# Edge counting moved between expert outputs and attention weights, expert rows added without order, x read back in chunks

## The chip, the cores and the metric

The kernel runs on one core of one Trainium2 chip. The metric is the device time of one execution in microseconds. Before the change the median of three executions is 2445.32 us (2440.54 to 2446.48).

## The reference

The model is four layers on a graph of N = 2708 nodes with D = 256 features and a dense 0/1 adjacency matrix. Each layer adds a graph part and then a feed-forward part to x, each on a layer norm of x:

```python
x = x + _L0_gnn_ref(ln(x), adj, ...)   # cosine attention over neighbours
x = x + _L0_ffn_ref(ln(x), ...)        # slice tokens and a small state-space scan
x = x + _L1_gnn_ref(ln(x), adj, ...)   # mean of neighbours, one linear map
x = x + _L1_ffn_ref(ln(x), ...)        # 8 experts, top 2, 256 -> 1024 -> 256
x = x + _L2_gnn_ref(ln(x), adj, W, a)  # graph attention, one head, elu
x = x + _L2_ffn_ref(ln(x), ...)        # 4 experts, scores from attention over an edge list
x = x + _L3_gnn_ref(ln(x), adj, W, a)  # graph attention, four heads
x = x + _L3_ffn_ref(ln(x), ...)        # 8 experts, top 1, with a capacity
```

The parts that matter here are the feed-forward of layer 1, the graph attention of layer 2, and one input of layer 2's feed-forward:

```python
# layer 1 feed-forward: a token's output is the weighted sum of its two experts
top_w, top_i = top_k(xf @ Wg + bg, 2); top_w = softmax(top_w)
out += w_dense[:, e:e+1] * (gelu(xf @ W1[e] + b1[e]) @ W2[e] + b2[e])

# layer 2 graph attention
wh = h @ W
e = leaky_relu(wh @ a1 + (wh @ a2).T, 0.2), masked by adj
h_prime = elu(softmax(e) @ wh)

# layer 2 feed-forward, scores: a segment softmax over 1,048,576 edges
src, dst = edge_index        # numbers below 65536, of which N are nodes here
```

Edge numbers are drawn below 65536, so only few edges have a destination among the 2708 nodes. The kernel has to find these edges in the list before layer 2's feed-forward.

## The kernel before

All of x stays in SBUF as 22 tiles of 128 rows (the last has 20). TensorE (PE) does the matrix products; VectorE (DVE) the layer-norm statistics, attention weights and copies; ScalarE (ACT) Gelu, exponentials and copies; GpSimd (POOL) starts the indirect DMAs; SyncE (SP) starts the plain loads. A scheduler fixes the order of instructions on each engine when the kernel is built: each engine then goes through its list in order, and an instruction that waits holds up what stands behind it. The order comes from the position in the program, which acts as a priority, and from the scheduler's own estimate of when operands are ready.

*Start.* The first four tiles of x are loaded singly, two by SP and two by ACT, then the rest in pieces of four or five tiles. `CHUNKS` are six pieces of 512 columns (the last of 148).

*Layer 1's feed-forward* (`fast_l1_ffn`). `Route` picks two experts for each token and writes, for every expert, a list of at most 768 rows (six tiles). An indirect DMA gathers an expert's rows (xe, L2954). Each expert is done in two halves of three tiles. A half is turned (xT: PE transposes, and copies from PSUM by `k.copy`, which alternates DVE, L76, and ACT, L78), goes up (h_ps, L3242, Gelu by ACT, L3249) and down (y_ps, L3259). DVE adds the bias and multiplies by the gate (ys, L3267 and L3268), and POOL adds the tile into rows of `acc` in DRAM by an indirect DMA (L3271). The adds write the same tensor, so each waits until the one before has landed. Rows of the lists that hold no token go to 128 spare rows behind the N + 1 rows of `acc`. PSUM has three banks for h_ps and two for y_ps. When all is added, x is read back from `acc` by SP.

*The edge search* (`Edges.search`, L2566 to L2590). The edge list is cut into eight pieces of 128x1024. For each piece DVE makes keys, then takes the eight largest of each row nine times (MAX8, L2585; the replacement, L2586), and reduces what is left (L2589). One piece is offered after each expert; the scheduler spreads the instructions between the outputs of experts, from 835 to 1065 us.

*The edge count* (`Edges.count`). A first part splits the found keys into node and row numbers, ranks the edges that are left over (rank_oh, L2686, rank_ov on POOL, L2701, 32 matmuls, L2708), and prepares `hib` and `lob`. Then 18 steps compare these with an iota: `oh` (128x4096, L2749), `ol` (128x704) and 32 small matmuls (L2756) that sum counts into cnt_ps. These steps are in the attention of layer 2, four after each chunk of columns; the scheduler moved the first part and two of the 18 steps up into the features before it.

*Layer 2's attention* (`fast_gat`, H = 1). First layer norm (L1617 to L1631), transposes (ft_ps, L1587), the features V and the two attention values of each node (v_ps, L3389; fs, L3399), an extreme of them (gx), and a spread of R over partitions (Rr). Then for each chunk of 512 target columns and each of 21 row tiles j: DVE makes PT (L3459), and PE does four matmuls (L3528) into four accumulators. PT has ten buffers, the adjacency tiles eight.

Of the kernel before, what the change touches and what calls it, by code (L numbers as in the profile page):

```python
# [1 line left out]

# [5 lines left out]
F32 = mybir.dt.float32  # L8
# [4 lines left out]
ALU = mybir.AluOpType  # L13
AX = mybir.AxisListType
PSUM = bass.MemoryType.PSUM
DRAM = bass.MemoryType.DRAM

N = 2708
# [25 lines left out]
class K:  # L44
# [3 lines left out]
    def __init__(self, ctx, tc, x_in):  # L48
        self.tc = tc
        self.nc = nc = tc.nc  # L50
        self.flip = 0
        pool = ctx.enter_context(tc.tile_pool(name="shared", bufs=1))
        self.x = pool.tile([128, NT, D], F32, name="x")
        nc.vector.memset(self.x[:, NT - 1, :], 0.0)
        for t in range(4):
            (nc.scalar if t % 2 else nc.sync).dma_start(
                self.x[:, t, :], x_in[t * 128 : (t + 1) * 128]
            )
        for t0, n in ((4, 4), (8, 4), (12, 4), (16, 5)):
            nc.sync.dma_start(  # L60
                self.x[:, t0 : t0 + n, :],
                x_in[t0 * 128 : (t0 + n) * 128].rearrange("(t p) d -> p t d", p=128),
            )
        nc.sync.dma_start(self.x[:TAIL, NT - 1, :], x_in[(NT - 1) * 128 : N])
# [5 lines left out]
        nc.vector.memset(self.eps, 1e-5)  # L70

    def copy(self, out, in_):
# [2463 lines left out]
class Edges:  # L2536
# [55 lines left out]
    def count(self):  # L2592
        nc, tc = self.k.nc, self.k.tc
        with tc.tile_pool(name="ep", bufs=1) as pp, tc.tile_pool(
            name="eh", bufs=2
        ) as hot, tc.tile_pool(name="ps_eh", bufs=1, space=PSUM) as ps:
            ioi = pp.tile([128, 128], I16, name="ioi")
# [51 lines left out]
            nc.vector.tensor_scalar(before, ioi, pc, None, ALU.is_gt)  # L2649
            rp = ps.tile([128, 5 * OW], F32, name="rank_ps")  # L2650
            bp = rp[:, 4 * OW : 4 * OW + 1]
# [91 lines left out]
            yield  # L2743
            cp = ps.tile([128, NT], F32, name="cnt_ps")
            for s0 in range(0, LW, HB):
# [89 lines left out]
class Route:  # L2835
# [14 lines left out]
    def __init__(self, k, ctx, w, most):  # L2850
# [9 lines left out]
        self.fd = dram.tile([N + 1, self.W], F32, name="fd")  # L2860
        self.acc = dram.tile([N + 1 + 128, D], F32, name="acc")
        self.idg = keep.tile([128, S], I32, name="idg")
# [66 lines left out]
        nc.vector.tensor_scalar(self.p1, self.own[:, 0:1], 1.0, None, ALU.add)  # L2929
        self.p1n = pool.tile([128, 1], F32, name="p1n")  # L2930
        nc.vector.tensor_scalar(self.p1n, self.p1, float(N), None, ALU.add)
        self.slot_f = pool.tile([128, 3, S], F32, name="slot_f")
# [31 lines left out]
    def early(self):  # L2964

        v = self.k.nc.vector
        bad = self.k.bad[:, 6:7]
        v.tensor_scalar(bad, self.sofar[:, 0:1], -1.0, float(HT * 128), ALU.mult, ALU.add)
        f = self.one.tile([128, 2, HT], F32, name="early_f")
        idf, idp = f[:, 0, :], f[:, 1, :]  # L2970
        v.scalar_tensor_tensor(
            idf, self.slot_f[:, 1, :HT], 128.0, self.slot_f[:, 2, :HT], ALU.mult, ALU.add
        )
        self.number(idf, idp, self.idg0, self.ids0)
        self.xe0 = self.gather(self.idg0, self.most * 128 + 1)
        yield

    def number(self, idf, idp, idg, ids):

        v = self.k.nc.vector  # L2980
# [217 lines left out]
def fast_l1_ffn(k, side, route, rest):  # L3198
# [8 lines left out]
    with ExitStack() as ctx:  # L3207
        dp = ctx.enter_context(tc.tile_pool(name="f1a", bufs=4))
        op = ctx.enter_context(tc.tile_pool(name="f1o", bufs=6))
        pst = ctx.enter_context(tc.tile_pool(name="ps_f1t", bufs=2, space=PSUM))  # L3210
        ps1 = ctx.enter_context(tc.tile_pool(name="ps_f11", bufs=3, space=PSUM))
        ps2 = ctx.enter_context(tc.tile_pool(name="ps_f12", bufs=2, space=PSUM))

        def psum():
            return pst.tile([128, 512], F32, name="xt_ps")

        class Half:
# [36 lines left out]
            def down(self):  # L3254
                _, _, w2t, b2t = route.weights[self.e]
                for i in range(HT):
                    y = ps2.tile([128, D], F32, name="y_ps")
                    for m in range(M):
                        nc.tensor.matmul(  # L3259
                            y,  # L3260
                            lhsT=self.hT[:, m, i * 128 : (i + 1) * 128],
                            rhs=w2t[:, m, :],
                            start=(m == 0),
                            stop=(m == M - 1),
                        )
                    ys = op.tile([128, D], F32, name="ys")
                    nc.vector.tensor_tensor(ys, y, b2t, ALU.add)  # L3267
                    nc.vector.tensor_scalar(  # L3268
                        ys, ys, self.xe[:, i, D + self.e : D + self.e + 1], None, ALU.mult
                    )  # L3270
                    nc.gpsimd.indirect_dma_start(  # L3271
                        out=acc,
                        out_offset=bass.IndirectOffsetOnAxis(
                            ap=self.ids[:, i : i + 1], axis=0
                        ),
                        in_=ys,
                        in_offset=None,
                        compute_op=ALU.add,
                    )
                    yield  # L3280

# [23 lines left out]
        route.slots()  # L3305
        side = side(route.start)
        nxt = [one, half(0, 1)]
        run(first)
        for e in range(E):
# [16 lines left out]
        for t0 in range(0, NT - 1, 3):  # L3326
            nc.sync.dma_start(
                k.x[:, t0 : t0 + 3, :],
                acc[1 + t0 * 128 : 1 + (t0 + 3) * 128].rearrange(
                    "(t p) d -> p t d", p=128  # L3330
                ),
            )
        nc.sync.dma_start(k.x[:TAIL, NT - 1, :], acc[1 + (NT - 1) * 128 : 1 + N])


def fast_gat(k, adjT, W, a, H, elu, col, side, parts=CHUNKS, after=None):
# [10 lines left out]
    with ExitStack() as ctx:  # L3347
# [109 lines left out]
        def product(PT, R, Q, aj):  # L3457

            nc.vector.scalar_tensor_tensor(PT, R, Q, aj, ALU.max, ALU.mult)  # L3459

        def weights(c0, cs, j, h, aj):

            PT = ptp.tile([128, 512], F32, name="PT")
            product(PT[:, :cs], Rr[:, h, c0 : c0 + cs], Q[:, h, j : j + 1], aj[:, :cs])
            return PT
# [51 lines left out]
        for i, (c0, cs) in enumerate(parts):  # L3517
            if H == 1:
# [24 lines left out]
                for (t, o, n), ac in zip(bl, acc):  # L3543
# [876 lines left out]
def part(I, prefix):  # L4420
    return {n[len(prefix) :]: ap for n, ap in I.items() if n.startswith(prefix)}


def model(tc, I, out):
# [4 lines left out]
    with tc.tile_pool(name="flags", bufs=1) as fp:  # L4429
# [4 lines left out]
        with ExitStack() as ctx:  # L4434
            k = Fast(ctx, tc, I["x"], bad, adjT)
            with ExitStack() as c0:
                pooling = Pooling(k, part(I, "L0_ffn_"), c0)
                fast_l0_gnn(k, adjT, I["L0_gnn_WqkT"], pooling)
                fast_l0_ffn(k, part(I, "L0_ffn_"), pooling)
            with tc.tile_pool(name="lists", bufs=1) as lp:  # L4440
                edges = Edges(k, part(I, "L2_ffn_"), lp)
                order = (0, 1, 5, 2, 3, 4)
                with ExitStack() as c1:
# [17 lines left out]
                    )  # L4461
                    fast_l1_ffn(k, edges.search, route, rest)
                fast_gat(
                    k, adjT, I["L2_gnn_W"], I["L2_gnn_a"], 1, True, 2, edges.count()
                )
# [75 lines left out]
```

## Time and profile before

The profiled execution took 2441.02 us; its span is 2439.3 us. Stages of the span, from the windows of the trace:

| stage | us | PE busy | DVE busy | TensorE clock |
|---|---|---|---|---|
| layer 0, graph part | 0 to 370 | 352.0 | 174.1 | 1.00 |
| layer 0, feed-forward | 370 to 600 | 206.7 | 147.9 | 0.90 |
| layer 1, graph part | 600 to 790 | 182.5 | 93.0 | 0.98 |
| layer 1, experts | 790 to 1165 | 355.1 | 269.7 | 0.98 |
| read-back and features of layer 2 | 1165 to 1233 | 36.7 | 51.8 | 0.76 |
| layer 2, attention | 1233 to 1456 | 220.5 | 207.6 | 0.99 |
| layer 2, feed-forward | 1456 to 1740 | 271.7 | 95.3 | 0.93 |
| layer 3, attention | 1740 to 2165 | 407.6 | 373.2 | 0.98 |
| layer 3, feed-forward | 2165 to 2439 | 227.8 | 124.7 | 0.90 |

A stage in which PE's busy time is near its length is bound by PE. A stage in which it isn't has waits, and the list of waits says for what. The clock is the share of full speed that TensorE was granted in the stage. In the profile's lines, `PE ft_ps L1587 <- DVE fa L1631: 19.1, 1, 19.1` means that PE, at the instruction that writes ft_ps on line 1587, waited for DVE's fa of line 1631: 19.1 us in total, once, 19.1 at the longest. A line of the timeline gives the start, the duration, the engine, the line, the operation, output and input, their shapes, how many instructions are merged, and in brackets the idle time before with what ended it.

### The profile page before, as it was taken

What the parts mean: (1) busy time and instruction counts of PE and PEld (TensorE: products, weight loads), DVE (VectorE), ACT (ScalarE), POOL (GpSimd) and SP (SyncE); (2) the same over time, 40 slices, a digit from 0 to 9 for tenths busy, and PEclk for the clock granted to TensorE, in tenths of its full rate; (3) what the DMA queues carried; (4) which work ended last, traced back from release to release, by engine and by line L of the source; (5) the groups of instructions that cost most, each with busy time, mean ns of one, the idle gap of its engine ahead of it and who ended that gap; (6) DMA issues with size and microseconds to landing.
All of it is one profiled execution on the core that took longest, in us unless ns stands there. A gap on an engine that the chain in (4) does not pass through costs nothing. (4 is left out here: it accounts for less than half of the span.)

```text
span 2439.3 us, 31809 instructions
## 1 busy us (share of the span) xinstructions
PE 2260.7 (93%) x11620; PEld 1509.5 (62%) x11620; DVE 1537.2 (63%) x3419; ACT 658.6 (27%) x1329; POOL 418.5 (17%) x490
## 2 busy tenths in 40 slices
PE   7999999988999899999599999999889999968997
PEld 4677775677877667767478867666653333325664
DVE  6444338655355699951698993252579999853544
ACT  5433333214663222121310013232321111111121
POOL 2000003005000333432150002520030000002221
PEclk9999999889999899999889996999899999978998
DMA  4233322200673444341254423000024443314340
GB/s 129 65 99 96 100 61 77 74 1 15 217 236 108 140 119 124 84 89 18 63 167 138 135 54 58 21 1 1 10 71 116 115 115 111 92 50 164 117 133 14
DMA packets 158380, 219.34 MB, mean 90 GB/s; under 512 B 30879, under 2 KB 94083, under 8 KB 158212
## 3 DMA queue, kind: packets, MB, share of 16 engines
q1 hardware_dynamic: 125856, 179.58, 25.7%
q0 software_dynamic: 15248, 23.39, 4.8%
q10 hardware_dynamic: 17108, 14.22, 1.8%
q8 instruction: 96, 1.57, 0.3%
q14 instruction: 72, 0.59, 0.1%
HBM read 193.49 MB, written 24.17 MB: 89 GB/s over the span
## 5 line engine op out<-in xcount | busy, mean ns | idle before, releaser
L3459 DVE SCALAR_TENSOR_TENSOR PT<-Rr,Q,aj 128x512 f32<-128x512 f32 (+3 forms) x630 | 406.1, 709 | 25.8 <-PE acc_ps L3528 13.9
L3605 PE MATMUL acc_ps<-PT,V 128*64 128x512 f32 (+4 forms) x2016 | 328.5, 549 | 0.4 <-ACT Rr L78 0.4
L3605 PEld LDWEIGHTS acc_ps<-PT,V 128*64 128x64 f32 (+1 forms) x2016 | 95.2, 122 | 210.2 <-issue 154.6
L1819 PE MATMUL acc_ps<-fa,PT 128*128 128x257 f32 x882 | 214.0, 382 | 0.5 <-DVE PT L1793 0.5
L1819 PEld LDWEIGHTS acc_ps<-fa,PT 128*128 128x128 f32 x882 | 164.6, 190 | 63.8 <-issue 41.0
L3528 PE MATMUL acc_ps<-V,PT 128*128 128x257 f32 x882 | 199.0, 385 | 1.5 <-POOL V L3416 0.9
L3528 PEld LDWEIGHTS acc_ps<-V,PT 128*128 128x128 f32 x882 | 167.6, 192 | 28.7 <-DVE PT L3459 2.4
L3242 PE MATMUL h_ps<-xT,w1t 128*128 128x384 f32 x512 | 173.4, 497 | 6.1 <-DVE xT L76 5.6
L1793 DVE SCALAR_TENSOR_TENSOR PT<-aj,PT 128x512 f32<-128x512 int32 (+1 forms) x126 | 80.2, 644 | 147.7 <-ACT PT L1792 147.6
L3259 PE MATMUL y_ps<-w2t,hT 128*128 128x256 f32 x768 | 168.6, 379 | 0.0
L2478 PE MATMUL acc_ps<-V,at 128*128 128x257 bf16 x1323 | 156.6, 277 | 3.7 <-DVE at L2472 3.7
L3259 PEld LDWEIGHTS y_ps<-w2t,hT 128*128 128x128 f32 x768 | 145.4, 190 | 21.4
L2478 PEld LDWEIGHTS <-at 128*128 128x128 bf16 x1323 | 129.4, 99 | 26.0 <-issue 5.0
L3242 PEld LDWEIGHTS h_ps<-xT,w1t 128*128 128x128 f32 x512 | 97.5, 194 | 73.9 <-DVE xT L76 7.3
L1792 ACT ACTIVATE PT<-s_ps,rq 128x512 f32<-128x512 f32 (+1 forms) x126 | 79.3, 636 | 168.1 <-PE s_ps L1768 167.0
L3271 POOL DMA_INDIRECT acc<-ys,ids x48 | 78.8, 1641 | 239.7 <-DVE ys L3268 114.1
L1768 PE MATMUL s_ps<-KT,QT 128*128 128x512 f32 (+1 forms) x252 | 116.4, 546 | 0.9 <-POOL KT L1747 0.6
L3951 PE MATMUL y_ps<-w2t,hT 128*128 128x256 f32 (+1 forms) x528 | 117.2, 379 | 0.0
L3938 PE MATMUL h_ps<-fT,w1t 128*128 128x512 f32 (+1 forms) x288 | 116.3, 554 | 0.1
L4374 PE MATMUL y_ps<-w2t,hT 128*128 128x256 f32 (+1 forms) x512 | 112.8, 379 | 0.0
L3951 PEld LDWEIGHTS y_ps<-w2t,hT 128*128 128x128 f32 (+1 forms) x528 | 97.7, 186 | 22.3 <-issue 8.2
L3249 ACT ACTIVATE hT<-h_ps,b1t 128x384 f32<-128x384 f32 x128 | 74.3, 580 | 110.3 <-PE h_ps L3242 107.8
(743 smaller groups left out, 3353.3 us busy)
## 6 DMA issues: line engine op xcount, KB each, us to landing
aj<-in_adjT SPq DMA_DIRECT2D x399, 256.0 KB
w1t<-in_L_ffn_W SPq DMA_DIRECT2D x8, 1024.0 KB
w2t<-in_L_ffn_W SPq DMA_DIRECT2D x8, 1024.0 KB
w1t<-in_L_ffn_w SPq DMA_DIRECT2D x8, 1024.0 KB
w2t<-in_L_ffn_w SPq DMA_DIRECT2D x8, 1024.0 KB
aj<-in_adjT SPq DMA_DIRECT2D x63, 74.0 KB
fd<-fa ACTq DMA_DIRECT2D x9, 512.0 KB
aj<-in_adjT SPq DMA_DIRECT2D x21, 202.0 KB
```

The lines of the kernel that those rows point to most:

```text
L1768: nc.tensor.matmul(s[:, :cs], lhsT=QT[:, j * 128 : j * 128 + 128], rhs=KT[:, c0 : c0 + cs], start=True, stop=True,)
L1793: nc.vector.scalar_tensor_tensor(PT[p, :n], aj[p, :n], 0.0, PT[p, :n], ALU.is_gt, ALU.mult)
L1819: nc.tensor.matmul(ac, lhsT=PT[:, o : o + n], rhs=fa[:, j, :], start=j == 0, stop=False)
L2478: nc.tensor.matmul(ac[:, c:], lhsT=at[:, o : o + n], rhs=V[:, j, r], start=j == 0 and q == 0, stop=False, skip_group_check=True,)
L3242: nc.tensor.matmul(hp, lhsT=w1t[:, kk, m * 128 : (m + 1) * 128], rhs=self.xT[:, kk, :], start=(kk == 0), stop=(kk == 1),)
L3259: nc.tensor.matmul(y, lhsT=self.hT[:, m, i * 128 : (i + 1) * 128], rhs=w2t[:, m, :], start=(m == 0), stop=(m == M - 1),)
L3459: nc.vector.scalar_tensor_tensor(PT, R, Q, aj, ALU.max, ALU.mult)
L3528: nc.tensor.matmul(ac[:n], lhsT=PT[:, o : o + n], rhs=V[:, j, 0, :], start=(j == 0), stop=False,)
L3605: nc.tensor.matmul(w.pop("out"), **w)
L3938: nc.tensor.matmul(o[:, :cs], lhsT=w1t[:, kk, m * 128 : (m + 1) * 128], rhs=fT[:, kk, c0 : c0 + cs], start=(kk == 0), stop=(kk == 1),)
L3951: nc.tensor.matmul(y[:n], lhsT=hT[:, m, o : o + n], rhs=w2t[:, m, :], start=(m == 0), stop=(m == M - 1),)
L4374: nc.tensor.matmul(y[:n], lhsT=hT[:, m, o : o + n], rhs=w2t[:, m, :], start=(m == 0), stop=(m == M - 1),)
```

## The change

1. `load_x` loads x at the start and reads it back after layer 1, in six pieces as `CHUNKS` has them (the last with a load of its own for the 20 rows). From the third on, each waits for the landing of the one two before it. All are on SP.
2. The adds of one expert are declared independent of each other; the first of an expert waits for all of the expert before; the read-back waits for the adds of the last expert. The spare rows of `acc` become 768, one for each row of a list, and are zeroed by six DMAs.
3. In layer 1's experts, h_ps has two PSUM banks and y_ps three. The copies of xT are all on ACT.
4. Search and count are one chain of steps. After experts 0 to 7 come 1, 1, 2, 1, 2, 1, 3 and 2 steps, each placed, by `tc.issue_after`, behind the last ys of that expert: eight of the search, the count's first part and four of the 18. The other 14 are in the attention, each behind the PT of every fifth row tile. The tiles of the count lie on the other side of the memories, and ranks and counts share one PSUM bank.

```diff
@@ Kernel
+        self.load_x(lambda r: x_in[r])
...
+    def load_x(self, src, also=None):
+        ld = []
+        for c0, cs in CHUNKS:
+            t0, n = c0 // 128, cs // 128
+            ld.append(
+                self.nc.sync.dma_start(
+                    self.x[:, t0 : t0 + n, :],
+                    src(slice(c0, c0 + n * 128)).rearrange("(t p) d -> p t d", p=128),
+                )
+            )
...
+        for i, inst in enumerate(ld):
+            if also:
+                also(inst)
+            if i > 1:
+                self.tc.add_manual_dep(
+                    inst.ins,
+                    ld[i - 2].ins.name,
...
@@ Route
-        nc.gpsimd.dma_start(self.acc[N + 1 :, :], zero[:, :D])
+        for i in range(TPE):
+            nc.gpsimd.dma_start(self.acc[N + 1 + i * 128 : N + 129 + i * 128, :], zero[:, :D])
...
-        v.tensor_scalar(idp, idf, 0.0, self.p1n, ALU.is_equal, ALU.mult)
+        spare = self.spare.rearrange("p e t -> p (e t)")[:, : idf.shape[1]]
+        v.scalar_tensor_tensor(idp, idf, 0.0, spare, ALU.is_equal, ALU.mult)
@@ fast_l1_ffn
-        ps1 = ctx.enter_context(tc.tile_pool(name="ps_f11", bufs=3, space=PSUM))
-        ps2 = ctx.enter_context(tc.tile_pool(name="ps_f12", bufs=2, space=PSUM))
+        ps1 = ctx.enter_context(tc.tile_pool(name="ps_f11", bufs=2, space=PSUM))
+        ps2 = ctx.enter_context(tc.tile_pool(name="ps_f12", bufs=3, space=PSUM))
...
-                    k.copy(self.xT[:, kk, :], tp[:, :HC])
+                    nc.scalar.copy(self.xT[:, kk, :], tp[:, :HC])
...
+                    mine = adds.setdefault(self.e, [])
+                    for o in mine:
+                        tc.declare_no_dep(add.ins, o.ins, reason="rows of other tokens")
+                    if not mine:
+                        wait_for(add, adds.get(self.e - 1, []))
+                    mine.append(add)
...
-            next(side)
-        for _ in side:
-            pass
...
+            with tc.issue_after(now[-1].last.ins):
+                for _ in range((1, 1, 2, 1, 2, 1, 3, 2)[e]):
+                    next(side)
+        k.load_x(lambda r: acc[1 + r.start : 1 + r.stop], lambda ld: wait_for(ld, adds[E - 1]))
@@ fast_gat
+                    if j % 5 == 4:
+                        with tc.issue_after(made[0].ins):
+                            next(side, None)
...
-                for _ in range(4):
-                    next(side, None)
```

More of the change, by code (lines that the diff above doesn't have):

```diff
@@ L1 @@
 from contextlib import ExitStack
+from itertools import chain
 import concourse.bass as bass
@@ L54, in __init__ @@
         nc.vector.memset(self.x[:, NT - 1, :], 0.0)
[L55 to L64, printed above, removed]
+        self.load_x(lambda r: x_in[r])
         self.ident = pool.tile([128, 128], F32, name="ident")
@@ L70, in __init__ @@
         nc.vector.memset(self.eps, 1e-5)
+    def load_x(self, src, also=None):
[8 more added lines that the diff above has]
+            )
+            if cs % 128:
+                ld.append(
+                    self.nc.sync.dma_start(
+                        self.x[:TAIL, NT - 1, :], src(slice((NT - 1) * 128, N))
+                    )
+                )
+        for i, inst in enumerate(ld):
[5 more added lines that the diff above has]
+                    ld[i - 2].ins.name,
+                    mybir.DependencyInfo(
+                        mybir.DependencyClass.Sync, mybir.DependencyReason.DATA
+                    ),
+                    reason="the first are to land first",
+                )
     def copy(self, out, in_):
@@ L2593, in count @@
         nc, tc = self.k.nc, self.k.tc
-        with tc.tile_pool(name="ep", bufs=1) as pp, tc.tile_pool(
-            name="eh", bufs=2
-        ) as hot, tc.tile_pool(name="ps_eh", bufs=1, space=PSUM) as ps:
+        with tc.tile_pool(name="ep", bufs=1, side="right") as pp, tc.tile_pool(
+            name="eh", bufs=2, side="right"
+        ) as hot, tc.tile_pool(name="ps_eh", bufs=1, space=PSUM, side="right") as ps:
+            bank = ps.tile([128, 512], F32, name="edge_ps")
             ioi = pp.tile([128, 128], I16, name="ioi")
@@ L2649, in count @@
             nc.vector.tensor_scalar(before, ioi, pc, None, ALU.is_gt)
-            rp = ps.tile([128, 5 * OW], F32, name="rank_ps")
+            rp = bank[:, : 5 * OW]
             bp = rp[:, 4 * OW : 4 * OW + 1]
@@ L2743, in count @@
             yield
-            cp = ps.tile([128, NT], F32, name="cnt_ps")
+            cp = bank[:, 5 * OW : 5 * OW + NT]
             for s0 in range(0, LW, HB):
@@ L2860, in __init__ @@
         self.fd = dram.tile([N + 1, self.W], F32, name="fd")
-        self.acc = dram.tile([N + 1 + 128, D], F32, name="acc")
+        self.acc = dram.tile([N + 1 + TPE * 128, D], F32, name="acc")
         self.idg = keep.tile([128, S], I32, name="idg")
@@ L2929, in __init__ @@
         nc.vector.tensor_scalar(self.p1, self.own[:, 0:1], 1.0, None, ALU.add)
-        self.p1n = pool.tile([128, 1], F32, name="p1n")
-        nc.vector.tensor_scalar(self.p1n, self.p1, float(N), None, ALU.add)
+        self.spare = count("spare", [E, TPE], [[0, E], [128, TPE]], base=N + 1, mult=1)
         self.slot_f = pool.tile([128, 3, S], F32, name="slot_f")
@@ L2966, in early @@
         v = self.k.nc.vector
-        bad = self.k.bad[:, 6:7]
-        v.tensor_scalar(bad, self.sofar[:, 0:1], -1.0, float(HT * 128), ALU.mult, ALU.add)
+        first = self.sofar[:, 0:1]
+        v.tensor_scalar(first, first, float(HT * 128), None, ALU.max)
         f = self.one.tile([128, 2, HT], F32, name="early_f")
@@ L3210, in fast_l1_ffn, with wait_for @@
         pst = ctx.enter_context(tc.tile_pool(name="ps_f1t", bufs=2, space=PSUM))
-        ps1 = ctx.enter_context(tc.tile_pool(name="ps_f11", bufs=3, space=PSUM))
-        ps2 = ctx.enter_context(tc.tile_pool(name="ps_f12", bufs=2, space=PSUM))
+        ps1 = ctx.enter_context(tc.tile_pool(name="ps_f11", bufs=2, space=PSUM))
+        ps2 = ctx.enter_context(tc.tile_pool(name="ps_f12", bufs=3, space=PSUM))
         def psum():
             return pst.tile([128, 512], F32, name="xt_ps")
+        adds = {}
+        def wait_for(inst, others):
+            for o in others:
+                tc.add_manual_dep(
+                    inst.ins,
+                    o.ins.name,
+                    mybir.DependencyInfo(
+                        mybir.DependencyClass.Sync, mybir.DependencyReason.DATA
+                    ),
+                    reason="all of an expert's rows",
+                )
         class Half:
@@ L3267, in down @@
                     nc.vector.tensor_tensor(ys, y, b2t, ALU.add)
-                    nc.vector.tensor_scalar(
+                    self.last = nc.vector.tensor_scalar(
                         ys, ys, self.xe[:, i, D + self.e : D + self.e + 1], None, ALU.mult
                     )
-                    nc.gpsimd.indirect_dma_start(
+                    add = nc.gpsimd.indirect_dma_start(
                         out=acc,
@@ L3305, in fast_l1_ffn @@
         route.slots()
-        side = side(route.start)
+        side = iter(side(route.start))
         nxt = [one, half(0, 1)]
@@ L3322, in fast_l1_ffn @@
                 k.checked()
-            next(side)
-        for _ in side:
-            pass
[L3326 to L3333, printed above, removed]
+            with tc.issue_after(now[-1].last.ins):
+                for _ in range((1, 1, 2, 1, 2, 1, 3, 2)[e]):
+                    next(side)
+        k.load_x(lambda r: acc[1 + r.start : 1 + r.stop], lambda ld: wait_for(ld, adds[E - 1]))
 def fast_gat(k, adjT, W, a, H, elu, col, side, parts=CHUNKS, after=None):
@@ L3457, in product @@
         def product(PT, R, Q, aj):
-            nc.vector.scalar_tensor_tensor(PT, R, Q, aj, ALU.max, ALU.mult)
+            return nc.vector.scalar_tensor_tensor(PT, R, Q, aj, ALU.max, ALU.mult)
+        made = [None]
         def weights(c0, cs, j, h, aj):
             PT = ptp.tile([128, 512], F32, name="PT")
-            product(PT[:, :cs], Rr[:, h, c0 : c0 + cs], Q[:, h, j : j + 1], aj[:, :cs])
+            made[0] = product(
+                PT[:, :cs], Rr[:, h, c0 : c0 + cs], Q[:, h, j : j + 1], aj[:, :cs]
+            )
             return PT
@@ L4440, in model @@
             with tc.tile_pool(name="lists", bufs=1) as lp:
+                side = []
                 edges = Edges(k, part(I, "L2_ffn_"), lp)
@@ L4461, in model, with search @@
                     )
-                    fast_l1_ffn(k, edges.search, route, rest)
+                    def search(start):
+                        side.append(chain(edges.search(start), edges.count()))
+                        return side[0]
+                    fast_l1_ffn(k, search, route, rest)
                 fast_gat(
-                    k, adjT, I["L2_gnn_W"], I["L2_gnn_a"], 1, True, 2, edges.count()
+                    k, adjT, I["L2_gnn_W"], I["L2_gnn_a"], 1, True, 2, side[0]
                 )
```

## The prediction

> **What bounds the kernel now.** Read in this order: page and stage windows, waits at the layer-1/layer-2 seam, then timelines of the two queues that the change reorders.
>
> ```profile
> PE 2260.7 (93%) x11620; PEld 1509.5 (62%) x11620; DVE 1537.2 (63%) x3419; ACT 658.6 (27%) x1329; POOL 418.5 (17%) x490
> ```
>
> TensorE is the bound in the mean. The windows (us, then busy time of PE, PEld, DVE, ACT, POOL, clock, DMA share) show where it isn't:
>
> ```profile
> 850.00:900.00 50.00, 47.31 (x194) 35.26 (x193) 50.00 (x74) 10.13 (x18) 14.48 (x12) 1.00 0.39 93
> 1100.00:1165.00 65.00, 64.56 (x270) 49.77 (x268) 9.92 (x24) 11.25 (x20) 15.75 (x10) 1.00 0.18 19
> 1165.00:1233.00 68.00, 36.71 (x193) 29.59 (x193) 51.84 (x158) 23.57 (x56) 15.32 (x19) 0.76 0.31 89
> 1233.00:1456.00 223.00, 220.47 (x1541) 185.20 (x1541) 207.59 (x318) 12.68 (x26) 23.83 (x33) 0.99 0.43 123
> ```
>
> In the expert FFN, DVE is full while it searches edges (850) and almost free later (1100); the seam and the features of layer 2 (1165 to 1233) leave PE idle for 31 us; in the attention (1233 on) PE is full, DVE nearly. Waits in 1160 to 1240 name the seam:
>
> ```profile
> PE ft_ps L1587 <- DVE fa L1631: 19.1, 1, 19.1
> DVE ln_st L1617 <- DMA x<-acc: 13.1, 1, 13.1
> POOL acc L3271 <- DMA acc<-ys,ids: 5.9, 2, 3.0
> PE cnt_ps L2756 <- DVE ol L2749: 3.1, 1, 3.1
> ```
>
> PE's last expert matmul ends at 1165.0; serial adds keep x from being read back. The last adds (POOL), then what DVE puts ahead of the attention (1224 on) and how long a search pair takes (859 on):
>
> ```profile
> 1166.83 1.56 POOL L3271 DMA_INDIRECT acc<-ys,ids  x1 [2.94 <-DMA acc<-ys,ids]
> 1171.35 1.57 POOL L3271 DMA_INDIRECT acc<-ys,ids  x1 [2.96 <-DMA acc<-ys,ids]
> ...
> 1224.00 4.80 DVE L2749 TENSOR_TENSOR oh<-io,lob 128x4096 bf16<-128x4096 bf16 x1
> 1228.72 1.28 DVE L76 COPY Rr<-spread_ps 128x512 f32<-128x512 f32 x2
> ...
> 859.23 2.35 DVE L2585 MAX8 L<-key 128x8 f32<-128x1024 f32 x2
> 863.86 2.36 DVE L2585 MAX8 L<-key 128x8 f32<-128x1024 f32 x2
> ```
>
> Two MAX8 with their replacements take 863.86 − 859.23 = 4.63 us of wall time, though the durations add up to 5.0: DVE instructions overlap by about 0.08, so I count starts, not durations.
>
> **The change, part by part.** The sum is against the profiled run's 2441.0 (span 2439.3); the median of three, 2445.3, stands 4.3 above it.
>
> *Start: −1.5.* PE's first matmul waits 13.5 us. Chunk 1 of x is awaited until 9.90, and the reciprocal of chunk 0 stands behind chunk-1 stats, at 11.44. With chunks 0 and 1 first and later ones held, both land near 5.5 by my estimate (1 MB at the 265 to 385 GB/s seen), and 16 stats end near 10. But chunk 0 as one 512 KB load lands later than 128 KB did (3.41), and later chunks wait for landings on SP, with layer 0's adjacency tiles queued behind them. Ends: −4 (stats no longer wait) and +2 (two landings exposed); PE's first s_ps at 30.3 rests on more than x, so −1.5.
>
> *Expert FFN: −3.5.* All xT copies go to ACT. PE waited for DVE's xT 3.5 + 2.1 us; ACT (0.48 a copy) has 89 busy of 375 us but runs Gelus of 0.58 ahead of it. Ends −5.6 and +3, taken −3. With adds no longer serial the first gathers of expert 1 stand less behind expert 0's adds; PE waited 7.3 for them; ends −2.8 (one 2.88 add wait) and 0, taken −1. h_ps with two banks instead of three is nothing: Gelu 0.58 lies inside a block of two matmuls, 1.3.
>
> The price is the search. In the static order of the changed kernel, search steps stand whole behind an expert's last output: 48 instructions before any output of expert 3, 49 before those of expert 5, and the last search rows, the count's first part and two one-hot steps before those of expert 7. PE can run ahead by three y banks, and by the next expert's up-projection that the order pulls forward (experts 4 and 6). From the end of expert 2 (T, about 945.5 in the old timeline), at 23.3 us per expert's up-projection (2 × 11.66) and 3.455 per y:
> - A step is 9 pairs of 2.315, a reduction 1.13 and five preparations 4.64: 26.6 us; two are 53.2. DVE is free for expert 3 at T + 0.8 + 53.2 = 54.0. PE has three y's at 33.7 and expert 4's up-projection to 54.7: no wait.
> - Expert 4's outputs and 14 interleaved instructions end at T + 90.5; 49 × 1.11 more: 144.8. PE wants expert 5's first y bank back at 88 + 33.7 + 23.3 = 145.0: at the edge.
> - Expert 6's outputs end near 179.7. Ahead of expert 7's: six search rows (6.7), twenty-odd count instructions at 0.37 to 0.73, two oh (4.33) and ol (0.80): 27, to 206.7. PE wants the bank at 176.2 + 33.7 = 209.9: 3 us to spare.
> I take +0.5. Ends: 0, and +11.5 if each step takes the sum of its durations (28.2): stalls of 1.4, 7.1 and 2.9.
>
> *Seam: +7.* The rank part of the count now lies among expert 7's outputs, so POOL's order there is adds 1 to 3, four rank_ov, adds 4 to 6. rank_ov waits for DVE L2684, behind output 5 and the 4.42 us rank_oh; by the same walk that ends 0.7 after PE's last y (before: 1165.0). Four rank_ov took 5.14 us; then three adds at 1.56 + 0.30 issue. The last lands about 2.3 after its issue (1172.9 to the x load at 1175.22): x is asked for at 14 ± 1 after PE's end, against 10.2 now, and the first 512 KB arrives 4 to 5 later, at 18 to 19. Meanwhile DVE has, ahead of any stats, rank copies that wait for the rank matmuls (7.2), 1.0 of small ones and two hot steps (10.3): free at 18 to 19 too. Then come pr/w (four of each, 2.7, now inside the features) and stats of two chunks (3.5) before the first fa: PE starts at about 26 instead of 19.05. Some 5 us of PE's count matmuls lie in this wait. Ends: −2 (adds freed, the 5.9 of waits gone, DVE not late) and +13 (below).
>
> *Features: −7.* Before, 25 us of count work was spread over 1201 to 1233. Without it: the Rr copies at 1228.72, which wait out the oh, come near 1224.8: 3.9; the fs copies blocked by the oh at 1206.93 cost PE 1.7; pr/w behind stats held PE 2.4, now paid at the seam; small ones in the chain from gx to R about 1. That is 9; I take 7 since some of it is hidden under PE's 3.1 us wait for ol, which goes too. Ends −10 and −3 (the Rr term alone).
>
> *Attention: −3.5.* 14 hot steps instead of 16, and no rank: 3 × 32 matmuls, 0.9 per 32, is 2.7 of PE; its waits for ol (1.9) go in part, since matmuls come later after each step. New: a hot step after every fifth PT. Five PT (0.665 apart) and one step (5.13) are 8.5 us of DVE, against 8.7 + 0.9 of PE: covered by ten PT buffers except in chunk 0, where PT takes 0.94: +1. Ends −5 and +3.
>
> Neutral: five more zeroing DMAs and an iota on POOL in layer 1's routing, where POOL has 126 of 375 us busy; the numbering keeps its instruction count but for one small one.
>
> Sum: −1.5 − 3.5 + 7 − 7 − 3.5 = −8.5, or 2432.5 against 2441.0. On the median's scale: 2437.
>
> **Two rules weighed.** At the seam PE rests 19 us and its granted clock in 1170 to 1187 was 0.50. The Trainium skill (TensorE: Matmul & The Clock Gate, Part 1) has the clock fall to half after about 3.4 us of idling, so 26 us of rest cost no more than 19; the count matmuls run at half speed inside the wait, and the sum stays. Against the change speaks another: two adds during search steps took 1.58 and 2.34 us, against 1.56 with DVE idle, and rank_ov beside PT ran with PT at 0.94 instead of 0.75. The skill (SBUF — State Buffer, SBUF: two separate sides) says that a two-port DVE operation shuts GpSimd out, DMA descriptors included, until it ends. By the rows an add under an oh costs under 1 us; by the rule adds 5 and 6 could each wait out a 4.4 us oh: the seam would be +13, the sum −2.5.
>
> **Rivals.**
> 1. *More gain* (chance 0.10): the seam only +3 and features −9: −14.5, 2431. For it: DVE and x are ready at about the same time, so neither adds; against: pr/w and 16 stats stand before the first fa.
> 2. *Search at its durations* (0.18): +11 more, 2448, no change. For it: the margin at expert 5 is 0.2 us; against: starts in the timeline, 4.63 a pair.
> 3. *Slower: outputs queued behind slower steps* (0.22). If search instructions take 15% longer beside the freed adds and gathers (30.6 a step), the same walk stalls PE by 7.7, 10.8 and 1.8: 20 us, the sum is +11.5, 2457. It decides from about 16 us of stall, a step of 29.5. For it: zero slack and an in-order queue; against: MAX8 ranged only from 1.205 to 1.265 beside the present adds.
> 4. *Adds held by oh at the seam* (0.10): +13 there, 2443, no change.
>
> **How the numbers follow.** The forecast has 0.40; with rival 1, faster by over 0.3% (7.3 us, about what a measurement tells from no change) has 0.50. Rivals 2 and 4 make 0.28 for the same, rival 3 0.22 for slower. The range runs from 2427 (rival 1 with the start at −4 and a little) to 2457 (rival 3); the forecast's own is 2430 to 2443.
>
> **What would show it.** Right: in the FFN, waits of PE for ys under 2 us, waits for xT nearly gone; at the seam, rank_ov between the adds, x loads 13 to 15 us after the last y, ft_ps waiting about 20 net of count matmuls; no oh between 1200 and 1233's counterpart; cnt waits under 2 in the attention. Wrong: y_ps or PE waiting for DVE's search rows at experts 3, 5, 7 (rivals 2, 3); POOL adds longer than 3 us behind oh (4); first ft_ps before 20 us (1).

## The result, and the profile after

The changed kernel takes 2431.11 us (median of 7; 2422.68 to 2434.38), before it 2444.61 (7 runs): a ratio of 0.9937 with a 95% interval of 0.9919 to 0.9955. That is faster by 0.6%, 13.5 us between the medians, where 8.3 was forecast. The profiled execution took 2434.38 us, span 2432.6. A second group of runs gave 2431.36, ratio 0.9950 (0.9933 to 0.9966).

The page's line of busy times (share of the span, instructions):

```profile
PE 2263.4 (93%) x11620; PEld 1512.2 (62%) x11620; DVE 1534.7 (63%) x3402; ACT 666.4 (27%) x1347; POOL 435.0 (18%) x496
```

The windows of the trace that answer to those shown of before (us; then busy time of PE, PEld, DVE, ACT and POOL; granted clock, DMA share, GB/s):

```profile
850.00:900.00 50.00, 49.52 (x201) 36.24 (x200) 36.90 (x52) 12.33 (x23) 19.93 (x15) 1.00 0.44 115
1100.00:1164.00 64.00, 62.47 (x263) 48.25 (x263) 63.53 (x110) 10.90 (x20) 26.66 (x19) 1.00 0.28 51
1164.00:1235.00 71.00, 38.49 (x319) 31.36 (x317) 43.28 (x140) 22.67 (x54) 17.70 (x20) 0.74 0.27 72
1235.00:1454.00 219.00, 214.74 (x1409) 180.37 (x1410) 188.31 (x279) 12.56 (x27) 26.79 (x27) 0.99 0.44 129
```

The busy times hardly fall: DVE has 2.5 us less, PE 2.7, ACT 7.8 and POOL 16.5 us more. Work has moved. DVE, which idled in the last 65 us of the experts, is full there now, and in the attention it is busy 188 us instead of 208. The seam and the features, 1164 to 1235, are *longer* than before, 71 us against 68, though the count's work on DVE in the features is gone. The waits in 1130 to 1240 and DVE's timeline say why:

```profile
PE ft_ps L1610 <- issue: 15.9, 1, 15.9
DVE pr L3414 <- DMA ar<-in_L_gnn_a: 9.4, 2, 9.1
PE edge_ps L2780 <- DVE ol L2773: 9.1, 2, 4.9
PE edge_ps L2732 <- POOL rank_ov L2725: 3.3, 1, 3.3
```

```profile
1156.93 4.42 DVE L2710 TENSOR_TENSOR rank_oh<-io,rlo 128x4096 bf16<-128x4096 bf16 x1
...
1162.80 3.18 DVE L2707 TENSOR_SCALAR rt<-si 128x32 int32<-128x32 int32 x1
...
1171.09 4.43 DVE L2773 TENSOR_TENSOR oh<-io,lob 128x4096 bf16<-128x4096 bf16 x1
...
1180.73 0.88 DVE L2773 TENSOR_TENSOR ol<-io,hib 128x704 bf16<-128x704 bf16 x1
1190.69 0.42 DVE L3414 TENSOR_TENSOR pr<-w,ar 128x256 f32<-128x256 f32 x1 [9.08 <-DMA ar<-in_L_gnn_a]
```

PE's last expert matmul ends at 1164.4. DVE is done with the count at 1181.6, x has been asked for at 1179.16, and then DVE stands for 9.1 us: `pr`, the product of W with the attention vector `ar` of layer 2, is ahead of the layer norm in its queue, and `ar` stands on SP behind x loads that wait for each other's landings. SP's own issues (the third x load, at 1183.18, waits for the first to land, so the first rows of x were there by then, 7.9 us before the first statistics):

```profile
1179.16 0.93 SPq L71 DMA_DIRECT2D x<-acc  x2
1180.31 0.37 SPq L3405 DMA_DIRECT2D w<-in_L_gnn_W  x1
1183.18 1.86 SPq L71 DMA_DIRECT2D x<-acc  x2
1185.09 0.50 SPq L3408 DMA_DIRECT2D ar<-in_L_gnn_a  x1
1187.15 3.46 SPq L71 DMA_DIRECT2D x<-acc  x2
```

The first ft_ps comes at 1198.53, 34.2 us after the last expert matmul; before it was 19.05. POOL's adds at the seam, which were 1.56 us each before:

```profile
1155.50 1.56 POOL L3311 DMA_INDIRECT acc<-ys,ids  x1 [1.09 <-DVE o_t L2637]
1157.37 5.42 POOL L3311 DMA_INDIRECT acc<-ys,ids  x1 [0.30 <-DVE rt L2697]
1162.54 3.38 POOL L2725 TENSOR_TENSOR rank_ov<-rank_oc,part 128x512 bf16<-128x512 bf16 x3
...
1169.69 1.56 POOL L3311 DMA_INDIRECT acc<-ys,ids  x1 [0.30 <-DVE deal L2740]
1171.55 5.39 POOL L3311 DMA_INDIRECT acc<-ys,ids  x1 [0.30 <-issue]
```

Two of them take 5.4 us, each beside a 128x4096 comparison on DVE (rank_oh from 1156.93, oh from 1171.09), and each ends 1.4 us after it.

**Where the time went**, read from the first and last instructions of the matmuls of each stage (us). "Free stretch" runs from the end of layer 0's attention to the first expert matmul; the change doesn't touch it, but for the first copy of xT. The other columns are runs of the next section. Each column is one profiled execution; that of "seam cleared" is the fastest of its six, 9.0 us under their median.

| stage | before | after | after again | start only | W by ACT | count late | seam cleared |
|---|---|---|---|---|---|---|---|
| start to end of layer 0's attention | 365.9 | 361.9 | 360.9 | 362.0 | 360.7 | 362.0 | 361.2 |
| free stretch | 427.9 | 434.9 | 432.1 | 431.7 | 427.7 | 435.1 | 427.5 |
| experts | 370.8 | 367.2 | 364.8 | 370.7 | 366.5 | 365.4 | 367.2 |
| seam and features | 68.2 | 71.1 | 71.4 | 67.8 | 66.7 | 56.8 | 55.4 |
| attention of layer 2 | 222.3 | 219.0 | 219.4 | 222.0 | 219.5 | 244.4 | 224.2 |
| to the first matmul of layer 2's experts | 39.6 | 37.5 | 37.0 | 39.5 | 34.2 | 34.5 | 32.0 |
| rest | 944.6 | 941.0 | 941.4 | 943.9 | 940.7 | 941.2 | 941.4 |

The profile pair differs by only 6.7 us, because before's profile had a short free stretch (427.9) and after's a long one (434.9). Without that row the pair differs by 13.7, near the 13.5 of the medians (the same count gives 16.5 for "after again", whose median is 14.0 below before): −4.0 at the start, −3.6 in the experts, +2.9 at the seam, −3.3 in the attention, −5.7 behind it.

### The profile page after: what moved, and what is told of

It reads as the page before. It is cut to its first block, busy times and chain, and to the rows that moved or that the text cites. A ratio compares the mean times of both kernels' runs of the same rounds, so it can differ in the third digit from the quotient of the medians.

```text
span 2432.6 us, 31798 instructions
## 1 busy us (share of the span) xinstructions
PE 2263.4 (93%) x11620; PEld 1512.2 (62%) x11620; DVE 1534.7 (63%) x3402; ACT 666.4 (27%) x1347; POOL 435.0 (18%) x496
## 3 DMA queue, kind: packets, MB, share of 16 engines
q1 hardware_dynamic: 126096, 179.84, 25.4%
q8 instruction: 96, 1.57, 0.3%
## 5 line engine op out<-in xcount | busy, mean ns | idle before, releaser
L3311 POOL DMA_INDIRECT acc<-ys,ids x48 | 86.2, 1796 | 216.3 <-DVE ys L3308 175.2
```

## The experiments

Ratios are to the kernel before, measured beside each run.

**start_only**: before, with `load_x` for the first load alone.

```diff
-        for t in range(4):
-            (nc.scalar if t % 2 else nc.sync).dma_start(
-                self.x[:, t, :], x_in[t * 128 : (t + 1) * 128]
-            )
...
+        self.load_x(lambda r: x_in[r])
```

> The kernel before with the chunked, gated loads of x at the start alone; the read-back and all else as before. If the start's gain is real and stays: the first s_ps near 27.1 us instead of 30.3, the end of layer 0's graph part 4 us earlier, and the time 3 to 4 us below before. If later stages swallow it (the clock of layer 0's feed-forward falling into another phase): the same first s_ps, and a time within 2 us of before.

Measured: 2438.57 us against 2445.51, ratio 0.9978 (0.9964 to 0.9991). First s_ps at 27.3 us, end of layer 0's attention at 362.0. The gain is real; by the trace it is 3.9 us, by the ratio 2 to 9.

**ar_act**: after, with W and the attention vector of layer 2 issued by ACT instead of SP.

```diff
-            nc.sync.dma_start(w[:, :, :D], W.rearrange("(k p) c -> p k c", p=128))
+            nc.scalar.dma_start(w[:, :, :D], W.rearrange("(k p) c -> p k c", p=128))
...
-                nc.sync.dma_start(
+                nc.scalar.dma_start(
```

> The changed kernel with the loads of layer 2's W and attention vector issued by ACT instead of by SP behind the held x loads. If the attention vector behind held x loads costs the seam 7 us or more: DVE's wait of 9.1 us for it is gone, the first ft_ps comes 27 us after the last expert matmul instead of 34.2, and the time is 6 to 8 us below the changed kernel. If the x rows themselves are the limit: DVE waits for x in its place, and the gain is under 2 us.

Measured: 2420.11 us, ratio 0.9904 (0.9883 to 0.9925), 8 to 11 us below the changed kernel (by its two ratios, 0.9937 and 0.9950; it did not run beside this one). DVE's wait for ar is 4.4 us instead of 9.1, and the first ft_ps comes 29.2 us after the last expert matmul instead of 34.2. Seam and features give 4.4 us, about what the wait lost (4.7); the rest is split over other stages (3 of it behind the attention) and was not traced to a cause. Two lines that say which engine issues three loads were worth more than half of the whole change.

**ar_e7_none**: the same, and no count steps after expert 7.

```diff
-                for _ in range((1, 1, 2, 1, 2, 1, 3, 2)[e]):
+                for _ in range((1, 1, 2, 1, 2, 1, 3, 0)[e]):
```

> The changed kernel with W and the attention vector loaded by ACT, and the two one-hot steps after expert 7 moved into the attention (16 there). If one-hot steps at the seam cost it twice, by DVE's time and by the adds they hold: adds 4 to 6 take about 1.6 each, x is asked for 9 to 11 us after the last expert matmul, the first ft_ps comes 17 to 20 us after it, and the time is 12 to 15 us below the changed kernel, with 2 given back in the attention. If only the attention vector mattered: the same as with that alone, 6 to 8 below.

Measured: 2424.45 us, ratio 0.9919 (0.9900 to 0.9937), 4 to 8 below the changed kernel; from W by ACT alone (0.9883 to 0.9925) the runs can't tell it apart. POOL's timeline of this run (rank_oh still stands beside the third add, no oh beside the last):

```profile
1157.88 5.18 POOL L3311 DMA_INDIRECT acc<-ys,ids  x1 [0.30 <-issue]
...
1168.09 1.57 POOL L3311 DMA_INDIRECT acc<-ys,ids  x1 [0.16 <-issue]
1169.97 1.56 POOL L3311 DMA_INDIRECT acc<-ys,ids  x1 [0.30 <-PE edge_ps L2732]
1171.84 1.56 POOL L3311 DMA_INDIRECT acc<-ys,ids  x1 [0.30 <-DVE odst L2756]
```

The adds did what was expected, and x was asked for 11.1 us after the last expert matmul. But the first ft_ps came after 25.5, not 17 to 20: DVE waited 10.8 us for ar. ACT issued W and ar only at 1175.84, beside x at 1175.60, presumably because their tiles take the memory of the experts' tiles, which is free when the last add has landed; no run tries this. So DVE's free time at the seam turned into a longer wait for ar: seam and features took 63.2 us, 3.5 less than with W by ACT alone, and two more steps lengthened the attention by 2.6 (222.1 against 219.5). The bound was what DVE waits for in front of the layer norm, not the amount of count work. Not all of the 10.8 us is ar's: x, if it took 3.8 us from its request to the first statistics as in the kernel before (1175.22 to 1179.00), would have been there at 1179.4, so by this estimate ar cost the last 3 us.

**count_late**: after, with the search alone in the experts and the whole count in the attention.

```diff
-                for _ in range((1, 1, 2, 1, 2, 1, 3, 2)[e]):
+                for _ in range((1, 1, 2, 1, 2, 1, 0, 0)[e]):
...
-                        side.append(chain(edges.search(start), edges.count()))
-                        return side[0]
+                        side.append(edges.count())
+                        return edges.search(start)
```

> The changed kernel with the whole count (first part and 18 steps) in the attention, behind every fifth PT, and only the search in the experts. If DVE's one-hot comparisons hold POOL's adds: without any of them near the adds, no add takes over 2.5 us (5.4 twice in the changed kernel), x is asked for about 6 us after the last expert matmul instead of 14.8, and the first ft_ps comes about 14 to 18 us after it instead of 34. If POOL's adds are slow for another reason, two stay above 5. The attention then carries 25 us more of DVE's count in its first chunk and two more... in all four more one-hot steps, and should be 8 to 18 us longer, so the time should lie within 8 us of the changed kernel.

Measured: 2438.62 us, ratio 0.9969 (0.9955 to 0.9984). All six adds take 1.55 us, x is asked for 4.9 us after the last expert matmul, the first ft_ps comes after 13.8 us. The attention takes 25.4 us more, beyond the 8 to 18 expected. PE's waits in 1218 to 1465:

```profile
PE acc_ps L3578 <- DVE PT L3502: 12.9, 3, 5.9
PE edge_ps L2732 <- POOL rank_ov L2725: 6.0, 1, 6.0
```

In the attention DVE is nearly full, so the count's first part there makes PE wait for PT. Moving the count between expert outputs pays, then: with the seam as bad as it is, it is still 5 to 8 us better than this (0.9950 and 0.9937 against 0.9969).

**control**: the changed kernel again.

> The changed kernel once more, beside the other runs of this group. 0.6% below before (0.992 to 0.9955). Its stretch from the end of layer 0's attention to the first expert matmul, which the change does not touch but for the first xT copy, took 434.9 us in the changed kernel's profile and 427.9 in before's; if that is the phase of TensorE's clock, it may be anything from 427 to 436 here.

Measured: 2431.36 us, ratio 0.9950 (0.9933 to 0.9966); its profile is the column "after again", with a free stretch of 432.1 us. The seam repeats: the first ft_ps comes 34.1 us after the last expert matmul, and the two held adds take 5.2 and 5.4 us.

**serial**: after, with the adds of an expert in order.

```diff
-                    for o in mine:
-                        tc.declare_no_dep(add.ins, o.ins, reason="rows of other tokens")
```

> The changed kernel with the adds of one expert in order again, each waiting for the one before. If the freed adds matter: the first gathers of expert 1 are late again (PE waits about 7 us for xe instead of 3.9), at the seam the last three adds take a pitch of 4.5 us or more and x is asked for 3 to 5 us later, and the time is 4 to 9 us above the changed kernel. If they are hidden: within 2 us of it.

Measured: 2433.51 us, ratio 0.9955 (0.9940 to 0.9970), 2.1 above the changed kernel beside it: no difference that the runs can tell. PE's wait for the first gathers is 3.6 us, as with free adds (3.9), so that wait did not shrink because of the adds. At the seam the order of POOL's work changes with the adds. The last two start at 1167.0 and 1174.4 and take 4.8 and 2.7 us, both beside an oh:

```profile
1167.01 4.82 POOL L3311 DMA_INDIRECT acc<-ys,ids  x1 [1.95 <-DMA acc<-ys,ids]
```

x is asked for 23.7 us after the last expert matmul instead of 14.8, but the first ft_ps comes only 2.1 us later (36.3 against 34.2): in the changed kernel DVE stands for ar in that time, here the first statistics stand ahead of pr, and it waits 7.1 us for x and only 1.4 and 1.2 for ar. Seam and features are some 4 us longer in the trace. The freed adds bring x forward by 9 us, and the wait for ar uses that up.

**xt_undo**: after, with xT copies shared by DVE and ACT and the old PSUM banks.

```diff
-        ps1 = ctx.enter_context(tc.tile_pool(name="ps_f11", bufs=2, space=PSUM))
-        ps2 = ctx.enter_context(tc.tile_pool(name="ps_f12", bufs=3, space=PSUM))
+        ps1 = ctx.enter_context(tc.tile_pool(name="ps_f11", bufs=3, space=PSUM))
+        ps2 = ctx.enter_context(tc.tile_pool(name="ps_f12", bufs=2, space=PSUM))
...
-                    nc.scalar.copy(self.xT[:, kk, :], tp[:, :HC])
+                    k.copy(self.xT[:, kk, :], tp[:, :HC])
```

> The changed kernel with xT copies shared between DVE and ACT and three banks for h_ps, two for y_ps, as before. If the third y bank is what lets PE run ahead of the queued search steps: PE reaches the full banks one y (3.455 us) earlier, the waits for ys at experts 3, 5 and 7 grow from 0.3, 2.4 and 0 to about 3.7, 5.9 and 0.5, copies of xT on DVE wait behind search instructions besides, and the time is 7 to 15 us above the changed kernel. If the banks do not matter: within 2 us.

Measured: 2500.26 us, ratio 1.0232 (1.0213 to 1.0251): 69 us above the changed kernel, where 7 to 15 were expected. PE's timeline at expert 3 (start, duration; in brackets the idle time before it and what ended it), and DVE's:

```profile
993.87 13.33 PE L3282 MATMUL h_ps<-xT,w1t 128*128 128x384 f32 x32 [35.60 <-DVE xT L99]
```

```profile
991.01 2.34 DVE L2612 TENSOR_REDUCE left<-key 128x1 f32<-128x1024 f32 x2
993.26 0.55 DVE L99 COPY xT<-xt_ps 128x384 f32<-128x384 f32 x1
```

The copy of xT stands in DVE's queue behind the reduction that ends two whole search steps, and PE can't begin the next up-projection without it: 35.6 us, twice.

**banks_undo**: after, with the old PSUM banks alone; xT stays on ACT. The diff is the first half of the one above.

> The changed kernel with three PSUM banks for h_ps and two for y_ps, as before; xT copies stay on ACT. This parts the two halves of the run that undid both and was 69 us slower. If the copies of xT on DVE, queued behind two search steps, made all of that (two waits of 35.6 us for xT): here PE loses only its third y ahead of the steps, the waits for ys at experts 3 and 5 grow from 0.3 and 2.4 to about 3.7 and 5.9, and the time is 5 to 9 us above the changed kernel (2431). If the third bank mattered as much: 30 us or more above.

Measured: 2438.08 us, ratio 0.9972 (0.9959 to 0.9985), 7 above the changed kernel (5 by the ratios), as expected. PE waits for ys three times, 1.8, 5.2 and 3.0 us, 10.0 in all against 2.7. So of the 69 us the copies on DVE made some 62 and the banks some 7. The 7 is what two stages leave: the experts take 382.2 us, 15 more than in the changed kernel, and seam and features 63.6, 7.5 less, with more of the count done before PE's last expert matmul (DVE is free of it 11.1 us after that instead of 17.2).

This pair of runs also answers a question that *serial* leaves. PE's wait for the first gathers is 6.9 us in xt_undo and 4.0 here, and the two differ in the copies of xT alone: with them on ACT, PE comes to the gathers later (idle from 821.3 instead of 819.2), and they land little sooner (825.3 instead of 826.1).

**best_c**: the seam cleared. The rank part of the count is traced last, after its 18 steps; first part and three steps after expert 6, none after expert 7; `pr` and `w` are traced with the first chunk of features.

```diff
-                for _ in range((1, 1, 2, 1, 2, 1, 3, 2)[e]):
+                for _ in range((1, 1, 2, 1, 2, 1, 4, 0)[e]):
...
             def project(c0, cs):
+                if c0 == 0:
+                    for kk in range(2):
+                        for s in range(2):
+                            pr = tmp.tile([128, H, Fo], F32, name="pr")
...
```

> The changed kernel with the seam cleared: the rank part of the count comes last, after its 18 steps; first part and three steps after expert 6, none after expert 7, 15 steps and the rank in the attention; the products of W and attention vector (pr, w) are traced with the first chunk of features instead of ahead of it. If the seam was lost to the held adds and to DVE's wait for the attention vector: no add at the seam over 2.5 us, x asked for 5 us after the last expert matmul, the first ft_ps 13 to 15 us after it instead of 34.2, 2 to 3 us given back at the first v_ps and 1 to 4 in the attention, where the rank stands behind PT: 12 to 18 us below the changed kernel, about 2415. If count work must be paid for wherever it stands: the attention grows by what the seam gains, and the time is within 3 us of the changed kernel.

Measured: 2419.60 us, ratio 0.9904 (0.9884 to 0.9924), 11.8 below the changed kernel beside it. Its PE timeline at the seam:

```profile
1143.12 13.20 PE L3298 MATMUL y_ps<-w2t,hT 128*128 128x256 f32 x60
1169.92 3.37 PE L1610 MATMUL ft_ps<-ident,fa 128*128 128x128 f32 x16 [13.60 <-DVE fa L1654]
1176.26 9.27 PE L3430 MATMUL v_ps<-w,fT 128*128 128x258 f32 x32 [2.98 <-DVE w L3421]
```

The last six adds take 1.55 us, x is asked for 4.8 us after the last expert matmul, the first ft_ps comes after 13.6. Seam and features fall to 55.4 us, and 4.8 come back in the attention.

**best_d**: the same, with no step at the first two places of the attention's first chunk.

```diff
-                    if j % 5 == 4:
+                    if j % 5 == 4 and (i or j > 9):
```

> The kernel with the cleared seam (rank last, three steps after expert 6 and none after expert 7, pr and w with the first features), and besides no step behind the first two places of the attention's first chunk, where PE waited 1.6 and 2.2 us for ol because few PT were made ahead. If these waits are the last cost of the count in the attention: they go, and the time is 2 to 4 us below the kernel with the cleared seam (2419.6), 0.988 to 0.990 of before. If the steps only move: the waits come back later in the attention, and the time is within 1.5 us of it.

Measured: 2419.36 us, ratio 0.9897 (0.9878 to 0.9916). The waits for ol fall from 3.8 to 0.9 us, and the wait for rank_ov grows from 1.5 to 4.2: the same time. About 2419.5 us, 1.0% below the kernel before, is the best that was reached; W by ACT alone, with 2420.11 and the same ratio as the cleared seam (0.9904), can't be told from it, though its seam and features took 11 us more in the profile. The two together were not run.

## Why the prediction was right, and where it was not

The direction, the outcome given the highest chance and the range (2427 to 2457) held; the gain was 13.5 us instead of 8.3. That the sum came so near is partly luck: seam and features together were 3 us worse than taken, the start 2.5 better, and 5.7 us came behind the attention, where nothing was expected. The 2431 measured is the number of rival 1 (chance 0.10), but not by its path, which had the seam at +3. Of the signs that were named, x was asked for in time (14.8 us) and no oh stands in the features; PE's waits for ys were 2.7 us and not under 2, its waits for xT 4.5 us and not nearly gone, and adds longer than 3 us behind oh, the sign of rival 4, came. Term by term, by the trace:

- *Start, −1.5 taken, −4.0 measured* (−5.0 in the control's profile), at the range's end or beyond. What was held back for landings exposed on SP did not come; start_only shows the gain by itself.
- *Experts, −3.5 taken, −3.6 measured* (−6.0 in the control's profile). The walk of DVE's queue was right in place: PE waits for ys 0.27 us at expert 3, 2.41 at expert 5 and not at expert 7, where none, an edge with 0.2 to spare, and none were worked out; in all 2.7, where 0.5 was taken. Counting starts, 26.6 us a step, was the choice that decided it; the sum of durations (rival 2) and slower steps (rival 3) are ruled out. The other two parts of the term were less well seen. PE's waits for xT fell by 4.6 us (4.5 for ACT, against 5.6 for DVE and 3.5 for ACT before), where 3 was taken. The wait for the first gathers shrank by 3.4, not 1, and not through the free adds (serial) but with the copies of xT (xt_undo and banks_undo), mostly because PE came to it later, which is little of a gain.
- What the prediction missed altogether is that the move of xT to ACT is not a small gain but what makes the queued search steps affordable. It priced the copies by their present waits, and did not ask what would stand in front of them in the new order. xt_undo does: 36 us, twice.
- *Seam, +7 taken, +15 measured* (34.2 against 19.05 us to the first ft_ps). DVE's end was worked out as 18 to 19 us after PE's and was 17.2; x was to be asked for at 14 ± 1 and was at 14.8; its first rows were to be there at 18 to 19 and were by 18.8 (SP's third x load, at 1183.18, waits for them). The step that failed is "Then come pr/w (four of each, 2.7) ...": it has the instructions and not what they wait for. The change puts waits on SP's x loads, and ar was queued behind them. ar_act, with that alone altered, is 8 to 11 us faster.
- Inside the seam the time at which x was asked for was right for a wrong reason. The four rank_ov were done 3.3 us after PE's end and not 5.8, and the last add lasted 3.8 us more than taken; the two misses nearly cancel. "By the rows an add under an oh costs under 1 us" was false: two adds took 5.4 us instead of 1.56. The row that it rested on is taken up below the list.
- *Features, −7 taken, −12.1 measured* (36.6 against 48.7 us from the first ft_ps to the first matmul of the attention). count_late and best_c, which have no count work there either but begin early, take 42.6 and 41.4 us: so the count's absence gave 6 to 7, as taken. The other 5 or so go with the late start, with 10 of the 22 statistics done when PE begins. Seam and features together were taken as 0 and are +2.9.
- *Attention, −3.5 taken, −3.3 measured* (−2.9 in the control's profile).
- *Behind the attention, 0 taken, −5.7 measured.* Of this 2.1 lies between the attention and the next experts, where all kernels with the new places of the count take 32.0 to 37.5 us, those with the old place 39.5 and 39.6. In these the last count work ends 12 us before the attention does, in the changed kernel 73 us before; that this is the cause was not tried alone. The remaining 3.6 lies in code that the change doesn't touch, and its cause is open.

**The adds beside oh.** The row from which the prediction took that an add under an oh costs little was this one, of the kernel before:

```profile
907.75 2.34 POOL L3271 DMA_INDIRECT acc<-ys,ids  x1 [5.07 <-DVE key L2586]
```

This add began while DVE ran a SCALAR_TENSOR_TENSOR of the search (L2577, from 907.43, 1.21 us) and ended 1.45 us after it, as the held adds end 1.4 us after their comparison. The row showed the same hold; it cost little because that operation is short. The rule of the Trainium skill weighed there (SBUF — State Buffer, SBUF: two separate sides) has GpSimd shut out until the DVE operation ends, if that is in a two-port mode, or has two inputs in SBUF while the GpSimd operation reads SBUF. The comparison has two inputs, io and lob; which of the two cases it is, no run here shows. That the adds are held, they do show: 5.42, 5.39 and 5.18 beside the three comparisons, 1.55 to 1.57 for the last adds of ar_e7_none and count_late with none beside. It holds the other way too: DVE's L2707, 0.16 us in serial with no rank_ov beside it, took 3.18 in the changed kernel and ended with the third rank_ov (1165.98 and 1165.92); in the kernel before it took 1.06, also beside a rank_ov. Rival 4 had the mechanism at a chance of 0.10. Its end, no gain, did not come: only one of the last three adds was held, and start, features and the stages behind gave more than was counted.

The other rule of the Trainium skill that was weighed, the clock's fall on idling (TensorE: Matmul & The Clock Gate, Part 1), agrees: the clock at the seam was 0.50 in 1170 to 1200 as it had been in 1170 to 1187, and with features of 36.6 us after the longer rest, no cost of it shows.

## What to carry to other kernels

Where work is queued behind a chosen instruction of an in-order engine, first move off that engine every small copy that another engine needs soon; here that one line, with the old banks in both, decided between 5 us gained (banks_undo) and 55 lost (xt_undo). When loads are made to wait for each other, list what else that queue carries and who needs it first: a 128 KB vector behind held loads cost 8 to 11 us, where the same order of loads brought 4 at the start. And a wait that the profile shows at a seam need not be the last one: with the last adds no longer held, DVE's wait for ar grew from 4.4 to 10.8 us, and the time did not fall.

## What the runs showed of the hardware

A 128x4096 bf16 comparison on VectorE holds an indirect add of GpSimd that begins while it runs, until it ends. Over the twelve profiles there are 14 such adds, and all ended 1.42 to 1.44 us after their comparison, whatever was left of it: they took 2.6 to 5.5 us instead of 1.55. Which operation runs matters: adds that began during a SCALAR_TENSOR_TENSOR of the search (1.2 us) also ended 1.42 to 1.57 us after it and took up to 2.65, while during MAX8, its replacement or TENSOR_REDUCE, of the same length, they took 1.54 to 1.66.

The free stretch of nearly unchanged work took 427 to 436 us from one profile to the next. Three windows of it in two kernels that do the same there, first with W by ACT (427.7 us in all), then ar_e7_none (435.3); the number before the DMA share is the clock:

```profile
455.00:485.00 30.00, 27.18 (x143) 21.48 (x144) 10.81 (x38) 4.58 (x8) 0.94 (x3) 0.62 0.47 149
485.00:520.00 35.00, 26.79 (x148) 21.46 (x147) 16.19 (x42) 7.16 (x12) 2.00 (x3) 0.69 0.01 1
607.00:636.00 29.00, 28.44 (x261) 24.80 (x264) 12.86 (x32) 25.95 (x73) 0.96 (x2) 1.00 0.99 338
```

```profile
456.00:486.00 30.00, 26.49 (x150) 19.95 (x149) 13.38 (x48) 5.21 (x10) 0.94 (x3) 0.77 0.46 149
486.00:521.00 35.00, 27.10 (x144) 23.30 (x145) 14.13 (x34) 6.47 (x11) 2.01 (x3) 0.61 0.00 1
609.00:640.00 31.00, 30.70 (x251) 25.93 (x252) 12.52 (x31) 26.60 (x74) 0.72 (x2) 0.90 0.94 310
```

The granted clock falls in other places each time, 0.62 or 0.77, 1.00 or 0.90 over nearly the same instructions. A change of this size can't be read from one pair of profiles: the pair said 6.7 us, the medians 13.5. Whether the phase of the clock alone makes the whole spread was not tried.
